# A four-layer convolution and attention chain: 64-output products in column halves, one instruction order to the end, and later corner arithmetic

## The chip, the cores and the metric

The kernel runs on one core of one Trainium2 chip. The metric is the device time of one execution in microseconds. Before the change three runs took 5382.01, 5395.89 and 5406.22 us; the median is 5395.89.

## What is computed

The input x is a batch of 2 images of 256 channels and 64 x 64 pixels, all in fp32. Four layers follow each other.

```python
# layer 0: group norm, 4-head attention over the 4096 pixels, projection
xn = group_norm(x); q, k, v = w_qkv @ xn
attn = softmax(q.T @ k * 64**-0.5);  x = xn + w_proj @ (attn @ v) + b_proj
# layer 1: position term
x = x + pos_embedding
# layer 2: bottleneck with a modulated deformable 3x3 convolution, 256 -> 64 -> 64 -> 256
h = relu(bn1(w1 @ x))
off, mask = conv3x3(h, woff)            # 18 offsets and 9 masks per pixel
samp = bilinear(h, pixel + tap + off) * sigmoid(mask)
h = relu(bn2(w2 @ samp));  x = relu(bn3(w3 @ h) + x)
# layer 3: two deformable 3x3 convolutions of 256 channels, with group norm and residual
h = relu(group_norm(x));  h = deform_conv(h, dw1, pw1, w1)
h = relu(group_norm(h));  x = x + deform_conv(h, dw2, pw2, w2)
```

## The kernel before

A batch has 4096 pixels, cut into NB = 8 blocks of 512. The program has two large parts.

**Attention** (line 160 on) goes through four units: two batches by two pairs of heads. A unit has 256 score tiles, each 128 queries by 1024 keys. The loop handles two tiles, n and n+1, per turn: scores of the tiles ahead (L569, TensorE), their row maxima (L581, VectorE), the exponentials (L587, ScalarE), 16 transposes of a finished tile (L599, TensorE) with two copies out of PSUM (L616 VectorE, L618 ScalarE), and the products with the values (L628, TensorE). Sixteen tiles make a block of 256 queries. Its four partial outputs are put together in `combine` (L508 to L514, on GpSimd), with factors `f` that go through DRAM (L498, L502). Two blocks make 512 queries, so 32 tiles are the period of the work around them. `project` (L533) then adds the projection to the residual, and, after the second pair of heads, `second_layer` calls `first` (L891).

Everything else in attention is background work, put between the tiles at due steps, or one step at a time from generators that `background` advances. A generator that yields "any", "a", "b" or True has used the turn; one that yields False passes it to the next generator. The background consists of:

- `first(b, i, ...)` (L891, L903): the product w1 of 64 outputs for one pixel block, and its copies to `h` with a row above and below.
- `before(b, ...)`: the transposed image of `h` in DRAM (L920, copy L924, four stores L929), the offset convolution (L938, copies L954 and L956, transposes by products L966), and the corner arithmetic (`corners`, L722 to L760), which yields gather indices `bidx` and weights `bw`. For batch 0 it runs in unit 1 and for batch 1 in unit 3.
- `conv(b, ...)`: gathers of four corners for each pixel and tap (L817 on GpSimd's queue), weighting (L1009, VectorE), sums (L1019, L1020, on GpSimd for batch 0 and on VectorE for batch 1), transposes (L1030), `second` (the product w2 of 64 outputs, L1039, five groups of taps), and `third` (the product w3, L1052, then L1056, L1059 and L1060 on VectorE). For batch 0 it runs in unit 2 and the start of unit 3.
- `early_image` (L1112 to L1134): batch 0's layer-3 image is written to DRAM; each block is loaded with `bott.block` (L873).

**Deform** (line 1138 on) is layer 3. Each step gathers four corners of 256 channels (L817, `four`), weights and adds them (L1305 ScalarE, L1311 VectorE), transposes (L1323), copies (L1332) and multiplies by the weights (L1342). The offsets come from `offsets`: weights `wf` (L1190, VectorE), products `pd` (L777, TensorE), a copy, shift products (L794), another copy (L803), transposes by products (L808) and the corner arithmetic. `conv` of batch 1 runs beside the first 160 or so steps; its gathers and layer 3's share GpSimd's queue.

**Order.** Both parts open a `manual_schedule` region of their own. Within a region TensorE, ScalarE, VectorE and GpSimd issue instructions in the order in which the program emits them. SP's queue is left to the scheduler, and so is the way in which the two regions' instructions are merged on one engine. PSUM for background work is one buffer, `pm`: the helper `ps` gives it out and first emits the copies that were put off for its previous use.

Of the kernel before, what the change touches and what calls it, by code (L numbers as in the profile page):

```python
# [18 lines left out]
P = 128  # L19
# [3 lines left out]
CM = 64  # L23
# [37 lines left out]
class Net:  # L61
# [39 lines left out]

    def zero_borders(self, zero):
# [67 lines left out]
    def attention(self, bott):  # L170
# [5 lines left out]
        with ExitStack() as ctx:  # L176
# [15 lines left out]
            engines = mybir.EngineType  # L192
            ctx.enter_context(
                tc.manual_schedule(
                    engines={engines.PE, engines.Activation, engines.DVE, engines.Pool}
                )
            )
# [241 lines left out]
            class Block:  # L439
# [66 lines left out]
                def combine(self):  # L506
                    o = self.o
                    nc.gpsimd.tensor_mul(o, o, self.f)  # L508
# [316 lines left out]
    class Bottleneck:  # L825
# [52 lines left out]
        def first(self, b, i, x, pools, ps):  # L878
# [10 lines left out]
            pc = ps([P, 512])  # L889
            for cb in range(2):  # L890
                nc.tensor.matmul(  # L891
                    pc[:CM], lhsT=self.w1[:, cb, :], rhs=x[:, cb, :],
                    start=(cb == 0), stop=(cb == 1),
                )
            where = [(rows(i), 1, 0, 8)]
# [5 lines left out]
            def copy():  # L901
                for dst, r, r0, n in where:
                    nc.scalar.activation(  # L903
                        dst[:, r * W : (r + n) * W], pc[:CM, r0 * W : (r0 + n) * W], AF.Relu,
                        scale=s[:CM, 0:1], bias=t[:CM, 0:1],
                    )
# [4 lines left out]
        def before(self, b, pools, ps):  # L911
# [5 lines left out]
            def image(i):  # L917
# [7 lines left out]
                for r in range(2):  # L925
                    for s in range(2):
                        y0 = 8 * i + r + 1 - s
                        dst = img[y0 : y0 + 7 : 2, 1 : W + 1, s, :].rearrange("j x c -> x j c")
                        nc.sync.dma_start(dst, t[64 * r : 64 * r + 64, :, :])  # L929

            def offsets(i):
# [29 lines left out]
                yield "any"  # L961
# [23 lines left out]
        def conv(self, b, pools, ps):  # L985
# [49 lines left out]
            def second(sts):  # L1035
                out = ps([P, 512])
                for g, st in enumerate(sts):
                    n = CM * len(self.GROUPS[g])
                    nc.tensor.matmul(  # L1039
                        out[:CM], lhsT=self.w2[:n, g, :], rhs=st[:n], start=(g == 0), stop=(g == 4)  # L1040
                    )
# [29 lines left out]
            for n, (i, g, js) in enumerate(steps):  # L1071
# [14 lines left out]
                if g == 4:  # L1086
                    del self.idx[b, i]
                    todo.append((n + 3, lambda sts=sts, h2=h2: h2.append(second(sts))))
                    for ob in range(2):

                        def out(i=i, ob=ob, x=x, h2=h2):
                            third(i, ob, h2[0], x)
# [4 lines left out]
                        todo.append((n + 4 + ob, out))  # L1097
# [5 lines left out]
    def early_image(self, bott, pools, ps):  # L1103
# [33 lines left out]
    def deform(self, bott):  # L1137
# [5 lines left out]
        with ExitStack() as ctx:  # L1143
# [10 lines left out]
            engines = mybir.EngineType  # L1154
            ctx.enter_context(
                tc.manual_schedule(
                    engines={engines.PE, engines.Activation, engines.DVE, engines.Pool}
                )
            )
# [381 lines left out]
```

## Time and profile before

| | us |
|---|---|
| median of three runs | 5395.89 |
| profiled execution | 5241.94 |
| its span, first to last instruction | 5240.2 |
| TensorE busy | 4868.1 (93%) |
| VectorE busy | 4207.5 (80%) |
| ScalarE busy | 2815.3 (54%) |
| GpSimd busy | 2246.8 (43%) |

The mean granted TensorE clock is 0.975. The profile names engines PE (TensorE matmuls), PEld (TensorE weight loads), DVE (VectorE), ACT (ScalarE), POOL (GpSimd) and SP (the DMA queue of SyncE); an ending q means the engine's queue or sequencer. Of the chain of work that ended last 65% lies on TensorE and 16% on VectorE. The costliest groups are L1311 on VectorE (1610.9 us), L587 on ScalarE (1145.9), L1342 on TensorE (1240.7) and L817 on GpSimd, as two groups of gathers (1155.0 and 580.2). In order of time attention ends near 2985 us, the last gather of layer 2's batch 1 is used near 3620, and the rest is layer 3.

### The profile page before, as it was taken

The page shows a single profiled execution, that of the slowest core. Times are in us where ns is not written, and L with a number is a line of the kernel's source. Part 1 is how long each engine was busy: PE and PEld are TensorE (multiplying, and loading weights), DVE is VectorE, ACT ScalarE, POOL GpSimd, SP SyncE. Part 2 cuts the span into 40 slices and gives each one's busy share as a digit, 9 for nine tenths or more (in the row PEclk, how much of TensorE's full clock was granted, in tenths as well). Part 3 has the DMA queues.
Part 4 walks back from the last instruction along what each step waited for, and adds up shares of the span by engine and source line. Part 5 has one row for each costly group of instructions (what it writes and reads, how often), then busy time and mean ns, then how long its engine had stood idle before and what let it go on. Part 6 is the DMA issues. An engine that isn't in the chain of part 4 may idle for free.

```text
span 5240.2 us, 99232 instructions
## 1 busy us (share of the span) xinstructions
PE 4868.1 (93%) x37976; PEld 2657.6 (51%) x37976; DVE 4207.5 (80%) x7922; ACT 2815.3 (54%) x5189; POOL 2246.8 (43%) x2241
## 2 busy tenths in 40 slices
PE   8999999999999999999999866667999999999998
PEld 5555565555555555655555523333444444444443
DVE  6878767787677787677677577777999999999998
ACT  5676656666566666666666422223444544444444
POOL 0111100010016676463000177776566566666665
PEclk9999999999999999999999988888999999999999
DMA  5221111111113333322511266667999999999998
GB/s 170 63 94 56 44 66 44 44 36 41 51 50 96 92 98 93 99 82 76 142 34 30 85 208 223 217 221 277 367 325 331 353 364 353 350 391 347 346 349 320
DMA packets 347147, 920.40 MB, mean 176 GB/s; under 512 B 58716, under 2 KB 98458, under 8 KB 346670
## 3 DMA queue, kind: packets, MB, share of 16 engines
q0 software_dynamic: 194688, 683.85, 36.8%
q1 hardware_dynamic: 151982, 230.20, 14.0%
q8 instruction: 298, 4.88, 0.4%
q14 instruction: 179, 1.47, 0.1%
HBM read 815.90 MB, written 89.60 MB: 173 GB/s over the span
## 4 chain that ended last, share of the span: by engine, by line
PE 65%; DVE 16%; DMA 6%; issue 6%; ACT 5%; POOL 3%; SPq 0%; ACTq 0%; DVEq 0%; POOLq 0%
PE av L628 15%; PE sc L569 14%; PE out L1342 10%; PE tt L599 9%; DVE smp L1311 8%; PE pd L777 5%; DMA four<-img,didx 4%; PE pt L1323 3%; POOL bfour L817 2%; DVE low L581 2%; ACT e L587 2%; PE pm L1039 1%; PE pm L271 1%; PE pm L533 1%; DMA bfour<-img,bidx 1%
## 5 line engine op out<-in xcount | busy, mean ns | idle before, releaser
L1311 DVE SCALAR_TENSOR_TENSOR smp<-four,dw,smp 128x256 f32<-128x256 f32 x3456 | 1610.9, 483 | 203.0 <-ACT smp L1305 120.3
L587 ACT ACTIVATE e<-sc,low 128x1024 f32<-128x1024 f32 x1024 | 1145.9, 1119 | 783.5 <-DVE low L581 780.4
L817 POOL DMA_INDIRECT four<-img,didx x1152 | 1155.0, 1003 | 665.5 <-DVE smp L1311 325.4
L1342 PE MATMUL out<-st,wc 128*128 128x512 f32 x2304 | 1240.7, 621 | 173.9 <-ACT st L1332 145.9
L581 DVE TENSOR_REDUCE low<-sc 128x1 f32<-128x1024 f32 x1024 | 1204.2, 1217 | 236.6 <-PE sc L569 234.0
L628 PE MATMUL av<-et,v 128*64 128x256 f32 x8192 | 1006.6, 386 | 0.0
L569 PE MATMUL sc<-k,qs 64*128 64x512 f32 x2048 | 998.4, 606 | 0.6 <-ACT e L587 0.3
L569 PE MATMUL sc<-k,q 64*128 64x512 f32 x2048 | 979.8, 605 | 0.0
L508 POOL TENSOR_TENSOR o<-o,f 128x1024 f32<-128x1024 f32 x64 | 151.6, 2369 | 1882.9 <-DVE o L463 872.5
L599 PEld LDWEIGHTS tt<-ident,e 64*128 64x128 f32 x16384 | 652.8, 139 | 526.9 <-issue 277.4
L1305 ACT ACTIVATE smp<-four,dw 128x256 f32<-128x256 f32 x1152 | 523.3, 503 | 460.4 <-DMA four<-img,didx 392.2
L599 PE MATMUL tt<-ident,e 64*128 64x64 f32 x16384 | 726.5, 226 | 47.1 <-DVE et L616 22.3
L618 ACT COPY et<-tt 128x512 f32<-128x512 f32 x1152 | 658.1, 584 | 166.5 <-PE tt L599 164.9
L616 DVE COPY et<-tt 128x512 f32<-128x512 f32 x896 | 611.0, 682 | 156.1 <-PE tt L599 155.9
L628 PEld LDWEIGHTS av<-et,v 128*64 128x64 f32 x8192 | 556.6, 137 | 308.6 <-issue 58.8
L1323 PEld LDWEIGHTS pt<-ident,smp 128*128 128x128 f32 x2304 | 321.8, 145 | 749.3 <-issue 426.2
L1332 ACT COPY st<-pt 128x1024 f32<-128x1024 f32 x288 | 290.7, 1009 | 722.0 <-PE pt L1323 722.0
L817 POOL DMA_INDIRECT bfour<-img,bidx x576 | 580.2, 1007 | 193.7 <-issue 93.2
L1342 PEld LDWEIGHTS out<-st,wc 128*128 128x128 f32 x2304 | 392.6, 197 | 437.6 <-issue 208.2
L1323 PE MATMUL pt<-ident,smp 128*128 128x128 f32 x2304 | 458.7, 282 | 72.9 <-DVE smp L1311 67.3
L777 PE MATMUL pd<-x,wf 128*126 128x512 f32 (+2 forms) x896 | 460.0, 599 | 10.6 <-DMA x<-xn 10.3
L569 PEld LDWEIGHTS sc<-k,qs 64*128 64x128 f32 x2048 | 346.1, 188 | 215.1 <-issue 118.1
(160 smaller groups left out, 3383.8 us busy)
## 6 DMA issues: line engine op xcount, KB each, us to landing
f<-share_d SPq DMA_DIRECT2D x128, 256.0 KB, 4.0
xb<-xn SPq DMA_DIRECT2D x55, 512.0 KB, 3.4
img<-imgt SPq DMA_DIRECT2D x96, 256.0 KB, 9.3
four<-img,didx POOLq DMA_INDIRECT x1152, 6.1
xa<-res SPq DMA_DIRECT2D x32, 512.0 KB, 2.9
xb<-in_x SPq DMA_DIRECT2D x20, 512.0 KB, 4.6
bfour<-img,bidx POOLq DMA_INDIRECT x576, 3.1
qs<-q SPq DMA_DIRECT2D x64, 128.0 KB, 2.2
```

Of the source, the lines that this page charges most:

```text
L569: nc.tensor.matmul(s[:, j, :], lhsT=q[u, i // 2][int(h != j)][halves[j], at : at + P], rhs=k[u][c][halves[j], h, :], start=True, stop=True,)
L581: nc.vector.tensor_reduce(low, s, AX.X, ALU.max, negate=True)
L587: nc.scalar.activation(e.rearrange("p j n -> p (j n)"), s, AF.Exp, bias=blk.low[:, g, c : c + 1], accum_out=blk.sum[:, g, c : c + 1],)
L599: nc.tensor.transpose(pt[:, m, :], e[half, m // 4, m % 4 * P : m % 4 * P + P], self.ident[half, half],)
L616: nc.vector.tensor_copy(dst, pt)
L618: nc.scalar.copy(dst, pt)
L628: nc.tensor.matmul(now["av"][halves[h], :], lhsT=v[u][c][:, m, halves[h]], rhs=ets[j][:, m, h, :], start=(m == 0), stop=(m == 7),)
L777: nc.tensor.matmul(pd[:m, r0 * W : r1 * W], lhsT=wt(s, t), rhs=src[:, (y + r0) * W : (y + r1) * W], start=(n == 0), stop=(n == len(srcs) * ...
L817: self.nc.gpsimd.indirect_dma_start(out=dst, out_offset=None, in_=img, in_offset=bass.IndirectOffsetOnAxis(ap=idx, axis=0),)
L1311: nc.vector.scalar_tensor_tensor(smps[s], four[:, c], weight(s, c), smps[s], ALU.mult, ALU.add)
L1323: nc.tensor.transpose(pts[u][:, c, j * P : (j + 1) * P], smp[:, c * P : c * P + P], self.ident,)
L1342: nc.tensor.matmul(outs[ob], lhsT=wc[k][:, c, ob * P : ob * P + P], rhs=sts[u][:, c, :], start=(k == 0 and c == 0), stop=(k == K2 - 1 and ...
```

## The change

1. In `first` and `second` the 512 columns are split into two halves of 256. The second half's 64 outputs go to the upper 64 partitions of a 256-column PSUM tile. Their copies become one activation per half, with scale and bias copied to the upper partitions at the start.
2. One `manual_schedule` region in `run` replaces the two, so the order of emission holds from attention's start to the end.
3. `combine` of the last block of the last unit runs on VectorE.
4. In `before`, corner arithmetic waits for 6 turns passed on (batch 1) or 1 (batch 0) in place of one used turn, and each image waits for one more. The last image's two stores for s = 1 go to ScalarE's DMA queue.
5. `third` is split: the product and L1056 in one step, L1059 and L1060 as `fourth` in the next.
6. `early_image` loads a block while the one before it is handled.

```diff
+        for v in (self.bn_s, self.bn_t):
+            nc.vector.tensor_copy(v[CM:P, 0:2], v[0:CM, 0:2])
...
-            engines = mybir.EngineType
-            ctx.enter_context(
-                tc.manual_schedule(
-                    engines={engines.PE, engines.Activation, engines.DVE, engines.Pool}
-                )
-            )
...
                 def combine(self):
+                    end = self.u + 1 == len(units) and self.i == 15
+                    engine = nc.vector if end else nc.gpsimd
                     o = self.o
-                    nc.gpsimd.tensor_mul(o, o, self.f)
-                    nc.gpsimd.tensor_add(o[:, 0:2], o[:, 0:2], o[:, 2:4])
+                    engine.tensor_mul(o, o, self.f)
+                    engine.tensor_add(o[:, 0:2], o[:, 0:2], o[:, 2:4])
...
-                    nc.gpsimd.tensor_add(self.av[:, half : half + 256], o[:, 0], o[:, 1])
+                    engine.tensor_add(self.av[:, half : half + 256], o[:, 0], o[:, 1])
...
-            pc = ps([P, 512])
+            pc = ps([P, 256])
             for cb in range(2):
-                nc.tensor.matmul(
-                    pc[:CM], lhsT=self.w1[:, cb, :], rhs=x[:, cb, :],
-                    start=(cb == 0), stop=(cb == 1),
-                )
-            where = [(rows(i), 1, 0, 8)]
+                for j in range(2):
+                    nc.tensor.matmul(
+                        pc[CM * j : CM * j + CM],
+                        lhsT=self.w1[:, cb, :],
+                        rhs=x[:, cb, 256 * j : 256 * j + 256],
+                        start=(cb == 0),
+                        stop=(cb == 1),
+                    )
+            where = [(rows(i), 1, 0, 4), (rows(i), 5, 4, 4)]
...
-                        dst[:, r * W : (r + n) * W], pc[:CM, r0 * W : (r0 + n) * W], AF.Relu,
-                        scale=s[:CM, 0:1], bias=t[:CM, 0:1],
+                        dst[:, r * W : (r + n) * W], pc[p, r0 * W : (r0 + n) * W], AF.Relu,
+                        scale=s[p, 0:1], bias=t[p, 0:1],
...
-                        nc.sync.dma_start(dst, t[64 * r : 64 * r + 64, :, :])
+                        queue = nc.scalar if b == 1 and i == NB - 1 and s else nc.sync
+                        queue.dma_start(dst, t[64 * r : 64 * r + 64, :, :])
...
                 yield "any"
-                yield "any"
+
+                for _ in range((1, 6)[b]):
+                    yield False
                 while len(self.idx) == self.CORNERS:
...
                 while self.blocks[b] <= i:
                     yield False
+                yield False
                 image(i)
...
             def second(sts):
-                out = ps([P, 512])
+                out = ps([P, 256])
                 for g, st in enumerate(sts):
                     n = CM * len(self.GROUPS[g])
-                    nc.tensor.matmul(
-                        out[:CM], lhsT=self.w2[:n, g, :], rhs=st[:n], start=(g == 0), stop=(g == 4)
-                    )
+                    for j in range(2):
+                        nc.tensor.matmul(
+                            out[CM * j : CM * j + CM],
+                            lhsT=self.w2[:n, g, :],
+                            rhs=st[:n, 256 * j : 256 * j + 256],
+                            start=(g == 0),
+                            stop=(g == 4),
+                        )
...
-                ps.later(
-                    lambda: nc.scalar.activation(
-                        h2, out[:CM], AF.Relu, scale=s[:CM, 1:2], bias=t[:CM, 1:2]
-                    )
-                )
+                def copy():
+                    for j in range(2):
+                        p = slice(CM * j, CM * j + CM)
+                        nc.scalar.activation(
+                            h2[:, 256 * j : 256 * j + 256], out[p], AF.Relu,
+                            scale=s[p, 1:2], bias=t[p, 1:2],
+                        )
+
+                ps.later(copy)
...
-                xs = x[:, ob, :]
-                nc.vector.scalar_tensor_tensor(
-                    xs, pc, s[:, 2 + ob : 3 + ob], xs, ALU.mult, ALU.add
-                )
+                nc.vector.scalar_tensor_tensor(
+                    x[:, ob, :], pc, s[:, 2 + ob : 3 + ob], x[:, ob, :], ALU.mult, ALU.add
+                )
+
+            def fourth(i, ob, x):
+                xs = x[:, ob, :]
                 nc.vector.tensor_scalar(xs, xs, t[:, 2 + ob : 3 + ob], 0.0, ALU.add, ALU.max)
                 nc.vector.bn_stats(self.stats[b][:, ob, i, :], xs)
...
-                        todo.append((n + 4 + ob, out))
+                        todo.append(
+                            (n + 4 + 2 * ob, lambda i=i, ob=ob, x=x, h2=h2: third(i, ob, h2[0], x))
+                        )
+                        todo.append((n + 5 + 2 * ob, out))
...
+        ahead = bott.block(pools["x"], x2d, 0)
         for i in range(NB):
-            x = bott.block(pools["x"], x2d, i)
+            x = ahead
+            if i < NB - 1:
+                ahead = bott.block(pools["x"], x2d, i + 1)
...
     def run(self):
         with ExitStack() as ctx:
             bott = self.Bottleneck(ctx, self)
+            engines = mybir.EngineType
+            ctx.enter_context(
+                self.tc.manual_schedule(
+                    engines={engines.PE, engines.Activation, engines.DVE, engines.Pool}
+                )
+            )
             self.attention(bott)
             self.deform(bott)
```

More of the change, by code (lines that the diff above doesn't have):

```diff
@@ L902, in copy @@
                 for dst, r, r0, n in where:
+                    p = slice(0, CM) if r0 < 4 else slice(CM, P)
+                    r0 %= 4
                     nc.scalar.activation(
-                        dst[:, r * W : (r + n) * W], pc[:CM, r0 * W : (r0 + n) * W], AF.Relu,
-                        scale=s[:CM, 0:1], bias=t[:CM, 0:1],
+                        dst[:, r * W : (r + n) * W], pc[p, r0 * W : (r0 + n) * W], AF.Relu,
+                        scale=s[p, 0:1], bias=t[p, 0:1],
                     )
@@ L1089, in conv, with out @@
                     for ob in range(2):
-                        def out(i=i, ob=ob, x=x, h2=h2):
-                            third(i, ob, h2[0], x)
+                        def out(i=i, ob=ob, x=x):
+                            fourth(i, ob, x)
                             if ob == 1:
@@ L1153, in deform @@
             pop = ctx.enter_context(tc.tile_pool(name="df_po", bufs=1, space=PSUM))
[L1154 to L1159, printed above, removed]
             T = DWK * DWK
```

## The prediction

> **What bounds the kernel now.** I read the page's slices first, then the busy times by stretch, then the order of time at the places that the change touches. The profiled execution took 5241.94 us (span 5240.2).
>
> ```profile
> PE   8999999999999999999999866667999999999998
> POOL 0111100010016676463000177776566566666665
> PEclk9999999999999999999999988888999999999999
> ```
>
> Each digit is one fortieth of the span, 131 us. TensorE is full everywhere but in slices 23 to 28 (about 2960 to 3660 us), where its granted clock is lower too. The stretches (columns: length, then busy time with the number of instructions of PE, PEld, DVE, ACT and POOL, then clock, DMA share, GB/s):
>
> ```profile
> 700.00:1400.00 700.00, 697.25 (x7642) 414.88 (x7639) 531.40 (x809) 446.77 (x835) 67.70 (x46) 1.00 0.15 44
> 1640.00:2260.00 620.00, 603.21 (x6309) 351.76 (x6310) 474.71 (x639) 390.47 (x727) 395.96 (x443) 1.00 0.31 94
> 2540.00:2960.00 420.00, 407.23 (x4303) 243.27 (x4303) 308.07 (x483) 277.93 (x520) 39.10 (x27) 0.99 0.18 47
> 3100.00:3660.00 560.00, 391.61 (x1113) 177.71 (x1114) 430.70 (x989) 153.65 (x268) 416.60 (x407) 0.84 0.70 232
> ```
>
> Attention is bound by TensorE: 97 to 99.6%, so TensorE time taken out there comes off the span. From 3013 to 3620 the bound is POOL: it issues one gather after another, 0.95 us each with 0.30 between that is put down to issue, and in order of time no gap above 0.45 us appears until 3623. There TensorE time is worth nothing. After 3660 TensorE leads again, with code the change leaves alone.
>
> **The column halves.** Three rows price them:
>
> ```profile
> 3003.75 1.93 PE L891 MATMUL pm<-res,w 128*64 128x512 f32 x4
> 2237.65 4.65 PE L1039 MATMUL pm<-bst,w 128*64 128x512 f32 x10 [0.63 <-ACT bst L1032]
> 2265.05 1.95 PE L628 MATMUL av<-et,v 128*64 128x256 f32 x16
> ```
>
> An fp32 product of 64 outputs by 512 columns is two instructions of 0.427 us, start to start (4.65 for ten). The attention's av products already have the form that the change introduces: 64 outputs, 256 columns, alternating between the two halves of the output partitions; sixteen take 1.95 us, so a pair takes about 0.213 and the halves run beside each other. L891 goes from 4 x 0.427 to 4 pairs x 0.213: 0.86 us less. L1039 goes from 10 x 0.427 to 10 pairs x 0.213: 2.13 less. A rule speaks against it: the Trainium skill, TensorEngine Tiling (Array Packing), "Instruction Overhead", puts about 60 cycles on every matmul, an estimate of 25 ns at the 2.4 GHz of its TensorE page. By that, 4 more instructions cost 0.10 and 10 more 0.25, leaving 0.76 and 1.88. The av row has its instructions' overhead in it, so I take 0.86 and 2.13. Fifteen L891 groups lie in full attention (the sixteenth in the tail below): 15 x 0.86 = 12.9. Eight L1039 groups (batch 0) lie there: 8 x 2.13 = 17.1. The other eight are under POOL's gathers: nothing. By the rule the two sums are 11.4 and 15.0. Bounds: 0 if halves run one after the other, 30 by the av row. Taken: **30.0**.
> The evacuations get one more ScalarE instruction each (64x512 becomes two of 64x256; 0.39 us is the price of the smallest form here); ScalarE is 63% busy beside it. Doubled weight loads run on PEld, 57% busy there. The two constant copies fall into the first 65 us, where DVE is busy 25. Nothing for these; without that cover 23 x 0.39 = 9 us.
>
> **Corners later.** The corner arithmetic of batch 1 now meets GpSimd's combination:
>
> ```profile
> 2942.22 2.34 POOL L508 TENSOR_TENSOR o<-o,f 128x1024 f32<-128x1024 f32 x1 [40.29 <-DVE pos L731]
> 2942.23 2.39 DVE L733 CAST whole<-pos 128x72 int32<-128x72 f32 x1
> 2944.65 1.30 DVE L736 CAST floor<-whole 128x72 f32<-128x72 int32 x1
> 2947.45 1.11 PE L599 MATMUL tt<-ident,e 64*128 64x64 f32 x15 [3.36 <-DVE et L616]
> 3015.35 0.20 DVE L733 CAST whole<-pos 128x72 int32<-128x72 f32 x1
> ```
>
> The same cast takes 2.39 us beside a POOL product and 0.20 alone (last row). VectorE's next copy of et is queued behind it, and TensorE waits 3.36 us. In the changed order corners come at tile 24 of each 32 in place of 19 (a tile is 2.7 us), past the combination at 20. What that is worth comes from equal blocks of batch 0 in unit 1, where corners stand at 22 and TensorE has no such wait: the chain of waits has L938 at 1214.93 and 1301.60, a block of 86.67; in unit 3, L271 at 2761.02 and 2849.84, a block of 88.82. 2.15 x 6 blocks = **12.9** (bounds 5 and 17). The image's step back by one turn moves its four stores on SP and one transpose group, not its length.
>
> **Image input ahead, and third split.**
>
> ```profile
> 2535.70 1.52 ACT L1112 ACTIVATE bx<-bx,gn_sh,gn_sc 128x512 f32<-128x512 f32 x2 [4.89 <-DMA bx<-x2d]
> 2537.74 1.59 PE L599 MATMUL tt<-ident,e 64*128 64x64 f32 x16 [4.98 <-ACT et L618]
> ```
>
> The load came too late once; ScalarE and then TensorE stood 4.98 us. In the new SP order each load stands a block earlier, ahead of the previous block's image stores. **5.0** (0 to 7). Splitting third puts L1056 on one step and L1059/L1060 (0.49 and 0.69) on the next, so that et copies aren't queued behind all three. In 1640 to 2260 TensorE idles 16.8 us from several causes; I take **3** (bounds -5 and 8: shifted steps can meet the combination anew).
>
> **One order to the end, last combination on VectorE, ScalarE's queue.** Before, the deformable layer's first work was woven into attention's tail:
>
> ```profile
> 2992.26 7.44 PE L777 MATMUL pd<-x,wf 128*126 128x512 f32 x12 [10.28 <-DMA x<-xn]
> 2999.62 1.08 PE L533 MATMUL pm<-avs,wproj 128*64 128x512 f32 x4
> 3012.97 1.03 POOL L817 DMA_INDIRECT bfour<-img,bidx  x1 [20.86 <-DMA img<-imgt]
> 3022.18 0.23 DVE L722 TENSOR_TENSOR pos<-pd,base 128x72 f32<-128x72 f32 x1 [1.82 <-PE pd L808]
> 3048.89 0.94 POOL L817 DMA_INDIRECT four<-img,didx  x1 [0.30 <-issue]
> ```
>
> The last projection stood behind twelve pd products. Now: factors land about 2984.4 (POOL's old start); three VectorE operations, an estimate of 2.4 from DVE rows of the same sizes (0.68 for 512, 0.42 for 256, about 1.25 for 1024); two projections with their additions, to 2990.6; L891 in halves, three activations, transposes, copy, to 2994.3; two image stores on SP beside two on ScalarE; landed about 2998. The 28 first gathers could start **15 us earlier**, and at 1.28 each end at 3034 against 3048.9.
> But the same order puts wf (3.43 on VectorE) and pd behind both corner blocks. From 2994.3: L938 2.8, its copies 2.1, L966 1.0, corners 4.0; the second block's L938 overlaps, then copies 2.1, L966 1.0, corners 4.0: 3011.7. Half of wf, 1.7; 28 pd instructions. TensorE idles before them, and the Trainium skill (TensorE: Matmul & The Clock Gate, "The HAM clock gate") says an idle window of about 3.4 us halves its clock until it has been busy as long: 8 instructions in 3.4 us and 20 x 0.427, 11.9. The row has 12 in 7.44, then 16 x 0.44: 14.5. I take the row. Then wide copy, shift products, od and sel: 5.9. L722 would run at about 3034, against 3022.18. On VectorE all but one of the early bfour sums are queued behind L722, and a gather of step 9 onward needs a buffer that these sums free: gathers 21 to 28 go out one or two per freed buffer, until 13.8 us after L722. The first four leaves about 3048, **1 us** earlier (bounds -8 and 14, the latter if POOL alone decides; by the rule 3.6). POOL's stage then moves as a whole.
> At its end POOL stood 8.01 us (3623.69) behind the last L1056; its L1039 is 2.1 shorter: **2** (0 to 5).
>
> **Sum.** 30.0 + 12.9 + 5.0 + 3 + 1 + 2 = 53.9 us off 5241.94: 5188. The median of the runs is 5395.89, 154 us above the profiled execution, for which the page shows no cause; I carry the gain over in proportion (x 1.029): 55.5, so 5340.
>
> **Rivals.**
> - *The halves don't overlap* (weight loads or a drain between them). For it: PEld loads double. Against: the av row. Then 23.9 x 1.029 = 25: 5371, within 0.5%. Chance 0.10.
> - *VectorE and ScalarE swallow half of the products' gain*: ACT waits for low 163 us in 1640 to 2260. Against: TensorE is 97% busy there all the same. 54 - 15 = 39: 5356. Chance 0.17.
> - *POOL alone decides the tail*: gathers at 3034, 13 us more: 5326. For it: the stage is POOL's. Against: the VectorE queue above. Chance 0.15.
> - *Slower: sums late for their transposes.* The batch 0 transposes wait for GpSimd's sums; one did, 1.82 us at 1657.73, behind the combination. Forty are in unit 2, and all move. At 1.82 each, 30 of 40 cancel the 54; stalls of 3 us at all forty give 120 - 54 = 66 slower: 5464. Against: only one stalls now, and the lag between sum and transpose is unchanged. Chance 0.06.
> - *My forecast*: 0.52.
>
> A measurement of this kernel tells about 0.5% (27 us) from no change. Faster by more 0.82 (forecast, swallowed half, POOL's tail, less their lower ends), within 0.11, slower 0.07. The range 5295 to 5378 goes from 1.9% below to just short of the rival in which halves don't pay plus the runs' own spread of 12 us.
>
> **What would show it.** L1039 as twenty instructions in about 2.4 us, L891 as eight in 1.1; blocks of unit 3 at 86 us or less; L733 at 0.2 there; no wait of ScalarE for bx; first bfour near 2998 less the attention's gain, first four some 36 to 50 later; POOL gapless in between or with a hole before gather 21. Wrong if the halves take 4 us, if TensorE's idle time in unit 2 grows over 17 us, or if the stage from the first four to the last L1039 gets longer than 576 us.

## The result and the profile after

| | before, us | after, us | ratio (95% interval) |
|---|---|---|---|
| the recorded comparison, 6 runs each | 5392.94 (5378.87 to 5406.22) | 5336.88 (5331.80 to 5348.98) | 0.9901 (0.9881 to 0.9922) |
| again, where before takes 5241 (5 runs of after) | 5240.94 | 5195.80 (5190.19 to 5203.13) | 0.9915 (0.9901 to 0.9929) |
| again, where before takes 5393 (5 runs of after) | 5393.46 | 5349.37 (5332.42 to 5358.58) | 0.9908 (0.9893 to 0.9922) |

The change made the kernel about 1% faster; 5340 had been predicted. The absolute times come in two sorts. On some chips before takes about 5242 us and on others about 5393. The profile of before (5241.94) was of the first sort, the profile taken of the changed kernel (5333.18) of the second. Each ratio below is of runs on one chip.

The page's slices of the changed kernel's first profile are these, each digit a fortieth of the span (133 us), in tenths.

```profile
PE   8999999999999999999999655566999999999998
...
POOL 0111101000027777461000566674566566666664
PEclk9999999999999999999999777788999999999999
```

Slices 23 to 28 are emptier than before, although nothing in the change makes the gathers slower. The stretches of the same profile, and below them those of the changed kernel on the other sort of chip (`a1_after`), show what the change did and what the chip did (columns: length, busy time with instructions of PE, PEld, DVE, ACT and POOL, then clock, DMA share, GB/s).

```profile
1640.00:2260.00 620.00, 604.24 (x6509) 358.63 (x6505) 480.15 (x655) 404.04 (x751) 405.16 (x452) 1.00 0.33 95
...
3100.00:3660.00 560.00, 325.55 (x1034) 145.18 (x1034) 373.99 (x861) 128.23 (x239) 379.24 (x371) 0.78 0.62 197
```

```profile
700.00:1400.00 700.00, 694.42 (x7728) 415.48 (x7726) 539.48 (x814) 453.93 (x845) 68.40 (x47) 1.00 0.16 45
1640.00:2260.00 620.00, 606.58 (x6561) 360.15 (x6557) 486.85 (x663) 405.77 (x756) 407.49 (x452) 1.00 0.33 98
2540.00:2960.00 420.00, 404.79 (x4302) 241.72 (x4302) 292.71 (x481) 275.63 (x516) 44.28 (x35) 0.97 0.19 55
3100.00:3660.00 560.00, 380.25 (x1266) 185.56 (x1266) 433.39 (x998) 171.27 (x299) 408.18 (x398) 0.83 0.74 245
```

In the gather stage (3100 to 3660) all engines together do less in the first profile: PE 326 us in place of 380, POOL 379 in place of 408, at 197 GB/s in place of 245. The last section comes back to that. To find what the change did, `a1_after` is set beside `b0_before`, a profile of before on a chip of the same sort. A unit is counted from the start of the last copy of partial sums (`o<-av` on VectorE, L463 before, L460 after) of one to that of the next, and attention ends with the last of them.

| us | before | after | difference |
|---|---|---|---|
| start to end of unit 0 | 753.9 | 754.9 | +1.0 |
| unit 1 | 713.9 | 710.8 | -3.1 |
| unit 2 | 761.4 | 741.0 | -20.4 |
| unit 3 | 755.8 | 728.2 | -27.6 |
| attention's end to the first gather `four` | 67.2 | 71.3 | +4.1 |
| first `four` to the last `second` | 571.7 | 573.4 | +1.7 |
| last `second` to the end | 1619.0 | 1614.4 | -4.6 |
| span | 5243.0 | 5194.0 | -49.0 |

(The other profile of before has 758.2 for unit 2: repeats lie some 3 us apart.) All of the gain was made in attention, 50.1 us of it, and the tail gave 4.1 back.

### The profile page after: what moved, and what is told of

Its sections match the earlier page's. It is cut to its first block, busy times and chain, and to the rows that moved or that the text cites. A ratio compares the mean times of both kernels' runs of the same rounds, so it can differ in the third digit from the quotient of the medians.

```text
span 5331.4 us, 99714 instructions
## 1 busy us (share of the span) xinstructions
PE 4839.4 (91%) x38200; PEld 2655.5 (50%) x38200; DVE 4190.9 (79%) x7927; ACT 2822.3 (53%) x5221; POOL 2238.2 (42%) x2238
## 4 chain that ended last, share of the span: by engine, by line
PE 37%; DVE 13%; issue 6%; another core or an unknown queue 3%; ACT 3%; POOL 2%; DMA 2%; SPq 0%; DVEq 0%; ACTq 0%; POOLq 0%
PE out L1365 11%; DVE smp L1334 8%; PE pd L777 6%; PE av L628 5%; PE sc L569 5%; PE tt L599 3%; PE pt L1346 3%; POOL bfour L817 1%; DVE bfour L1020 1%; DVE low L581 1%; DMA four<-img,didx 1%; PE pd L794 1%; ACT st L1355 1%; ACT smp L1328 1%
## 5 line engine op out<-in xcount | busy, mean ns | idle before, releaser
L628 PE MATMUL av<-et,v 128*64 128x256 f32 x8192 | 994.9, 385 | 0.0
```

The source lines that it names most:

```text
L628: nc.tensor.matmul(now["av"][halves[h], :], lhsT=v[u][c][:, m, halves[h]], rhs=ets[j][:, m, h, :], start=(m == 0), stop=(m == 7),)
```

## The experiments

The three runs of unchanged kernels come first. They are the ones that the others are measured against.

`b0_before` is before itself: 5244.72 us, span 5243.0.

> The kernel before, profiled once more, because its first profile (5242 us) lies 150 us below its own median while the changed kernel's profile (5333) lies on its median. Theory A: ordinary runs of the kernel before lose those 150 us in the stage of layer 2's batch-1 gathers, where the changed kernel's profile shows every engine at rest together for 7 to 30 us, waiting for something the profile can't name: then attention ends again at 2982 +- 2 us, the stretch from the first layer-3 gather to the last w2 product is 640 us or more (576 in the first profile), and the whole is 5380 to 5405. Theory B: the loss is spread over the execution (a lower clock): then attention ends 60 us or more later and the stretch stays below 600.

It was on a chip where before takes 5242 again (attention's end at 2985.0, the stage from the first `four` 571.7), so it tests neither theory on what the slower runs lose.

`a0_after`, the changed kernel on a chip where before takes 5393: 5349.37, ratio 0.9908.

> The changed kernel again, to stand beside the versions with one part undone. If a part's worth can be read as a difference on one chip: attention ends near 2949 as in its first profile, 7 us before the full-width version (2956.7) and 10 us before the version with early corners (2959.3); the whole is near 5207 where the kernel before takes 5242, and slower than the version with two regions (5191). If instead the ratio of the first measurement (0.990) holds here: 5190, and attention has to end 15 us before 2949 or the tail has to be shorter, because nothing waits unexplained here.

`a1_after`, the changed kernel where before takes 5241: 5195.80, ratio 0.9915.

> The changed kernel, unchanged, beside the two-region version on one chip. Theory A (one order costs the tail): attention ends within 5 us of the two-region version, the first gather of layer 3 (`four`) starts 71 to 74 us after attention's end against 63 to 66 there, and the whole is 7 to 12 us slower than with two regions. Theory B (one order changes attention too): attention also ends 7 to 13 us later than with two regions, and the whole is 15 to 22 us slower. Theory C (the tail is made good by POOL's stage): the two differ by under 3 us.

### Full width again, in the changed kernel

```diff
-                for j in range(2):
-                    nc.tensor.matmul(
-                        pc[CM * j : CM * j + CM],
-                        lhsT=self.w1[:, cb, :],
-                        rhs=x[:, cb, 256 * j : 256 * j + 256],
...
+                nc.tensor.matmul(
+                    pc[:CM], lhsT=self.w1[:, cb, :], rhs=x[:, cb, :],
...
```

(and the same in `second`)

> The changed kernel with the two 64-output products back in full width (512 columns, one half of the partitions, one activation each). The prediction's sum: attention ends 30 us later than the changed kernel's 2949.4, near 2979, and the whole is 30 us slower, near 5367, nothing of it from the gather stage. Rival, half swallowed: PE saves 30 us of products but waits more for the copies of the transposed tiles; attention ends near 2962 (12 us later) and the whole is 10 to 15 us slower unless the gather stage adds its own.

Measured: 5221.76 (5218.15 to 5226.72), ratio 0.9963 (0.9949 to 0.9976), against 0.9915 with the halves. Units 1 to 3 took 715.1, 749.5 and 738.7 us, so against `a1_after` the halves are worth 4.3, 8.5 and 10.5 us there, 23.3 together, and 26.0 by the medians (the two runs are of two chips, on which before takes 5242 and 5241). The prices of one group are as they were read from the av row. In order of time on TensorE, `a1_after` (L1051) and the first profile after (L893) have

```profile
2222.13 2.48 PE L1051 MATMUL pm<-bst,w 128*64 128x256 f32 x20
```

```profile
1119.23 1.08 PE L893 MATMUL pm<-res,w 128*64 128x256 f32 x8
```

Twenty instructions in 2.48 us where ten took 4.65, eight in 1.08 where four took 1.93: the two halves of the output partitions do run beside each other. That the whole is 23.3 and not the 30.0 that these prices give is not in the products themselves. Over units 1 to 3 (columns as above) `a1_after` has the first of these lines and `e1_full_width` the second:

```profile
754.90:2934.90 2180.00, 2141.93 (x23292) 1282.11 (x23292) 1667.46 (x2507) 1448.01 (x2696) 702.89 (x729) 1.00 0.24 68
```

```profile
753.40:2956.70 2203.30, 2171.50 (x23152) 1284.58 (x23152) 1664.38 (x2507) 1435.80 (x2673) 700.40 (x729) 1.00 0.24 68
```

TensorE's busy time is 29.6 us shorter, nearly the 30.0, but its idle time grew by 6.3, from 31.8 to 38.1. Of this, 5.3 us are waits for ScalarE's copies to `h` (L910). `e1_full_width` has no such wait of TensorE, and `a1_after` has these in attention (columns: what was waited for, us in total, times, longest):

```profile
PE pm L491 <- ACT h L910: 2.4, 9, 0.3
PE pm L1153 <- ACT h L910: 1.0, 1, 1.0
PE pm L287 <- ACT h L910: 1.0, 1, 1.0
PE pm L1073 <- ACT h L910: 0.9, 1, 0.9
```

They are products of other background work that use the buffer `pm` next, and the copies to `h` have to leave it first.

### The halves alone, in before

```diff
+        for v in (self.bn_s, self.bn_t):
+            nc.vector.tensor_copy(v[CM:P, 0:2], v[0:CM, 0:2])
...
-            pc = ps([P, 512])
+            pc = ps([P, 256])
...
-                out = ps([P, 512])
+                out = ps([P, 256])
```

(with the products and copies in halves, as in the change, and nothing else of it)

> The kernel before with nothing but the column halves (and the two constant copies they need). The prediction's sum: 13 us in the w1 products and 17 in unit 2's w2 products, attention ends at 2953 +- 3 in place of 2983, the whole is 30 us faster, 5212. Rival, swallowed: TensorE then waits for the copies of the transposed tiles (PE before L599) for half of it or more; attention ends at 2968 or later, the whole is 8 to 15 us faster, and the stage of batch-1 gathers stays at 572 +- 3 us.

> The halves alone, once more, for a profile to set beside before's units (713.9, 761.4 and 755.8 us from last partial sum to last partial sum of units 1, 2 and 3). In the first run of it unit 1 took 717.5, unit 2 757.8 and unit 3 755.7; the changed kernel's unit 2 took 758.8 beside it and 741.0 on another chip, so 18 us of unit 2 may be the chip's. Theory A (halves lose in units 1 and 3 to the image's wait for h, and pay in unit 2): if before takes about 5242 on this chip, unit 1 is 717 to 718, unit 2 739 to 745, unit 3 755 to 756, attention ends near 2968, ratio 0.996 to 0.998. Theory B (halves pay nowhere without the later image): unit 2 takes 755 or more on such a chip too, attention ends near 2984, ratio 0.999 or more.

Measured: 0.9977 (0.9963 to 0.9991) and 0.9989 (0.9981 to 0.9996), both on chips where before takes 5393. That is 6 to 12 us, far from 30. Unit 1 took 717.5 us in both, 3.6 more than before, and unit 3 took 755.7 and 756.2, no less than before's 755.8. Unit 2 took 757.8 and 759.6. It takes 758.8 in `a0_after` too and 741.0 in `a1_after`, so its length on these chips says nothing of the halves, and these two runs do not settle the second run's theories on unit 2. Another run speaks for the first: `e3_corners_early` (below) has the halves with corners and image at their old turns, where before takes 5242, and its unit 2 takes 742.0, within the first theory's 739 to 745. It also has the split and the loading ahead, but these change unit 2 by 1.0 us only (759.8 without them, 758.8 with them, in `e6_no_split_no_ahead` and `a0_after`). On units 1 and 3 the first theory is confirmed. The waits of attention in `e10_halves_again`, where L929 is the image's transposes and L912 the copies to `h` (L920 and L903 before), have

```profile
PE pm L929 <- ACT h L912: 20.3, 14, 2.3
```

Before has 1.7 us in two such waits. One of the 14 in order of time, in the same kernel:

```profile
1120.47 1.08 PE L895 MATMUL pm<-res,w 128*64 128x256 f32 x8
...
1123.33 1.96 ACT L912 ACTIVATE h<-pm,bn_t,bn_s 64x256 f32<-64x256 f32 x4
...
1125.35 0.40 PE L929 MATMUL pm<-ident,h 64*128 64x64 f32 x3 [1.43 <-ACT h L912]
```

and the same place in `b0_before`:

```profile
1121.33 1.35 ACT L903 ACTIVATE h<-pm,bn_t,bn_s 64x512 f32<-64x512 f32 x3
...
1122.74 0.40 PE L920 MATMUL pm<-ident,h 64*128 64x64 f32 x3
```

ScalarE's copies to `h` are four instructions of 1.96 us in place of three of 1.35, and the transposes of the image come right behind them on TensorE, which stands still. TensorE gains 0.85 on the product and gives 1.43 back; that is 0.6 us a block, the 0.61 by which the copies are longer, and six such waits make up the 3.6 us of unit 1. The Trainium skill states this in TensorEngine Tiling (Array Packing), "PSUM Bottleneck": packing the array speeds up TensorE but not the copies out of PSUM, which may then bind. Here they bind where TensorE stands directly behind them, although ScalarE as a whole was busy only 63 to 66% in attention's stretches of before.

### The halves and the image one turn later, in before

```diff
                 while self.blocks[b] <= i:
                     yield False
+                yield False
                 image(i)
```

> Before with the column halves and, of the later order, only the image's one turn. Halves alone ended attention at 2984.7, no earlier than before, with 18 us of TensorE waits of the image's transposes for ScalarE's last copy of h. Theory A (these waits ate the halves' gain): the transposes wait under 4 us in all, attention ends at 2966 to 2973, and the ratio to before is 0.994 to 0.996. Theory B (the halves' gain in attention is eaten by slower steps elsewhere, not by this wait): the wait goes but attention ends at 2980 or later, ratio 0.997 or more.

Measured: 5204.92 (5201.48 to 5207.70), ratio 0.9931 (0.9917 to 0.9945). That is 36 us, above the 21 to 31 of theory A, and theory B is out; no wait of the transposes for `h` is left. (Other products still wait for these copies, 8.0 us in attention against 1.0 with the halves alone.) (Attention's end at 2942.0 is far before A's 2966 to 2973, since those were counted from 2984.7 of a chip whose unit 2 is 17 us longer.) Units 1 to 3 took 711.8, 740.7 and 734.5 us. The one `yield False` takes 5.7 us from unit 1 and 21 from unit 3 (against the halves alone; these two units take the same in `a0_after` and `a1_after` within 0.7 us, so they can be set beside each other across the chips). More than went with the waits for `h` was gained, and the next two experiments show what else.

### The later order alone, and the later order taken out

In before, at full width, the corners and the image are made later:

```diff
                 ps.later(lambda: copy((0, 1)))
                 yield "any"
-                yield "any"
+
+                for _ in range((1, 6)[b]):
+                    yield False
...
+                yield False
                 image(i)
```

> Before with only the later corners and the later image: full width, two regions, no split, no loading ahead, combination on GpSimd. By the prediction's term it takes 12.9 us off: attention ends near 2970, unit 3's blocks take 86 to 87 us (88.8 before), ratio 0.9975. If the image's turn alone matters when there are halves, and the corners' term is as sized, the same. If the corners' term was too large (corners meet the combination elsewhere), attention ends at 2976 or later and the ratio is 0.999 or more.

Measured: 5226.84 (5221.83 to 5234.72, 9 runs), ratio 0.9977 (0.9967 to 0.9987): 14.1 us where 12.9 had been predicted, and unit 3's equal blocks take 86.7 us (88.8 before). Its profile, the fastest of the nine runs, has unit 3 at 743.5, some 12 us less than before, and unit 2 at 750.2, 8 to 11 us less. The prediction has no term for unit 2. There the two edits overlap: the later order alone brings it to 750, the halves without it to 742.0 (`e3_corners_early`), both to 741. Then the opposite, both edits taken out of the changed kernel:

```diff
-
-                for _ in range((1, 6)[b]):
-                    yield False
+                yield "any"
...
-                yield False
                 image(i)
```

> The changed kernel with corner arithmetic and images at their old turns (one used turn, no turn passed on). The prediction's sum: the corners of batch 1 meet GpSimd's combination again, 2.15 us in each of six blocks, attention ends 13 us later, near 2962, and the whole is 13 us slower. Rival: with halves and split steps the positions have shifted anyhow and the meeting does not recur: attention ends within 3 us of 2949.4.

Measured: 5219.38 (5215.31 to 5222.37), ratio 0.9955 (0.9941 to 0.9969): 21 us slower than the changed kernel by the ratios, 23.6 by the medians, where 13 had been expected, and unit 3's blocks take 89.4 to 89.7 us. In order of time on GpSimd, VectorE and TensorE, `e3_corners_early` has

```profile
2651.57 2.35 POOL L508 TENSOR_TENSOR o<-o,f 128x1024 f32<-128x1024 f32 x1 [42.56 <-DVE o L460]
...
2652.28 1.69 DVE L731 TENSOR_SCALAR pos<-pos 128x72 f32<-128x72 f32 x1
...
2654.01 1.31 DVE L733 CAST whole<-pos 128x72 int32<-128x72 f32 x1
...
2655.97 0.71 PE L599 MATMUL tt<-ident,e 64*128 64x64 f32 x15 [1.53 <-DVE et L616]
```

and the halves with the image's turn alone, `e7_halves_image_later`, where the same lines are L511, L734 and L736,

```profile
2647.71 2.35 POOL L511 TENSOR_TENSOR o<-o,f 128x1024 f32<-128x1024 f32 x1 [40.96 <-DVE o L466]
...
2652.73 0.19 DVE L734 TENSOR_SCALAR pos<-pos 128x72 f32<-128x72 f32 x1
...
2652.95 0.20 DVE L736 CAST whole<-pos 128x72 int32<-128x72 f32 x1
```

In `e3_corners_early` the corner arithmetic runs into GpSimd's product, and the two instructions shown take 1.69 and 1.31 us; TensorE then waits 1.53 for VectorE. In `e7_halves_image_later` the offsets come after the image, so its one turn has carried the corners along: from L734 on they run 2.7 us after GpSimd's product ended and take 0.19 and 0.20. Unit 3's blocks are 86.4 us there and 86.2 in the changed kernel. **The image's one turn is enough for both jobs**: it frees the transposes from the copies to `h`, and it moves the corners off the combination. The corners' own further turns save another 0.2 us a block and the one meeting that is left in `e7_halves_image_later` (L736 takes 1.31 us at 2907.5, and TensorE waits 1.52). The corners' turns without the image's, and the image's turn at full width, were not run.

### No split of third, no loading ahead

```diff
-            x = ahead
-            if i < NB - 1:
-                ahead = bott.block(pools["x"], x2d, i + 1)
+            x = bott.block(pools["x"], x2d, i)
...
-                        todo.append((n + 5 + 2 * ob, out))
+                        todo.append((n + 4 + ob, out))
```

(and L1082 and L1083 back in `third`)

> The changed kernel without the split of the w3 step and without the image input a block ahead. The prediction's sum: 5 us for the input, 3 for the split: attention ends 8 us later than the changed kernel's. In the profile ScalarE waits about 5 us for bx once again. Rival: the loads are hoisted by the scheduler of SP's queue anyhow and the wait falls elsewhere; attention ends within 2 us of the changed kernel's.

Measured: 5360.85 (5356.85 to 5376.45), ratio 0.9943 (0.9930 to 0.9957), against 5349.37 and 0.9908 of `a0_after` on the same chip: the two edits together are worth 11.5 us, where 8 had been expected, and 12.7 in unit 3 (741.0 against 728.3). In order of time `e6_no_split_no_ahead` still has before's late load, and `a0_after` the rest of it:

```profile
2538.20 1.52 ACT L1133 ACTIVATE bx<-bx,gn_sh,gn_sc 128x512 f32<-128x512 f32 x2 [4.58 <-DMA bx<-x2d]
```

```profile
2529.51 1.52 ACT L1141 ACTIVATE bx<-bx,gn_sh,gn_sc 128x512 f32<-128x512 f32 x2 [1.19 <-DMA bx<-x2d]
```

The load's wait costs more than itself. Behind it TensorE stood 4.68 us, and from 2538 to 2544 its granted clock in `e6_no_split_no_ahead` was 0.50, some 3 us more (an estimate, half of the 6); `a0_after` has 1.00 in all of 2520 to 2560. Over unit 3 `e6_no_split_no_ahead` has the first of these lines and `a0_after` the second:

```profile
2225.50:2966.50 741.00, 714.57 (x7588) 428.56 (x7584) 543.64 (x851) 497.12 (x923) 183.82 (x187) 0.98 0.24 68
```

```profile
2224.40:2952.70 728.30, 709.98 (x7586) 425.69 (x7582) 542.24 (x852) 497.12 (x923) 183.60 (x187) 1.00 0.25 69
```

Of the 12.7 us, 8.1 are idle time of TensorE (26.4 and 18.3), and 4.6 are longer work at a lower clock. The two edits were not run apart, so how the rest divides between them stays open. Nor is it certain that they bring this much without the corners' own turns. `e7_halves_image_later` has neither the two edits nor those turns, and its unit 3 takes 734.5, 6.5 us less than here. It differs from `e6_no_split_no_ahead` in the order to the end as well, but with two regions or one the changed kernel's unit 3 lies between 728.2 and 731.8. So the split and the loading ahead probably make good in part what the corners' turns cost.

### Two regions again, in the changed kernel

```diff
     def run(self):
         with ExitStack() as ctx:
             bott = self.Bottleneck(ctx, self)
-            engines = mybir.EngineType
-            ctx.enter_context(
-                self.tc.manual_schedule(
...
```

(and a region each for attention and deform, as before)

> The changed kernel with a region of fixed order for each part again, so that the deformable layer's first products can be woven into attention's tail. The prediction: the tail's two effects cancel, the first layer-3 gather leaves 1 us later than in the changed kernel (72 us after attention's last copy), the whole is unchanged within 5 us. Rival, fixed order costs: woven in, wf and pd run during the projection's waits and keep TensorE's clock up; the first layer-3 gather leaves 55 to 62 us after attention's last copy, the whole is 10 to 17 us faster. A third possibility, that the new position of the gathers sets the stalls of the stage: then the stage's length changes by tens of us with attention unchanged.

> The changed kernel with the two regions of before. Its ratio to before is 0.990 by the earlier run of it; under A the changed kernel's ratio beside it is 0.9915 to 0.9925, under B 0.993 to 0.994, under C within 0.0006 of it. In the profile: first gather of `four` some 64 us after attention's end, and L722 some 43 us after it.

Measured: 5191.03 (5186.05 to 5192.77), ratio 0.9899 (0.9884 to 0.9914), and 5189.04 (5183.25 to 5193.77), ratio 0.9900 (0.9884 to 0.9915). Beside the second run the changed kernel took 5195.80. The intervals overlap; the two profiles show where the 6.8 us between the medians lie. Attention ends at 2934.8 and 2934.9, the stage from the first `four` on takes 573.6 and 573.4, and between the two the first `four` starts after 63.9 us with two regions and after 71.3 in one order. The changed kernel's tail in order of time:

```profile
2940.43 1.97 PE L533 MATMUL pm<-avs,wproj 128*64 128x512 f32 x4 [5.54 <-DVE avs L514]
...
2945.94 1.98 PE L893 MATMUL pm<-res,w 128*64 128x256 f32 x8 [0.79 <-DVE res L544]
...
2950.77 5.43 PE L946 MATMUL pm<-h,woff 64*96 64x512 f32 x6 [0.52 <-DVE imgt L931]
...
2975.35 12.78 PE L777 MATMUL pd<-x,wf 128*126 128x512 f32 x28 [5.06 <-DVE wf L1213]
...
2985.50 0.95 POOL L817 DMA_INDIRECT bfour<-img,bidx  x1 [0.30 <-issue]
...
2992.72 0.23 DVE L722 TENSOR_TENSOR pos<-pd,base 128x72 f32<-128x72 f32 x1 [15.05 <-PE pd L808]
...
2995.32 0.94 POOL L817 DMA_INDIRECT bfour<-img,bidx  x1 [8.88 <-DVE floor L740]
```

With two regions (pd is L783, the projection L539):

```profile
2945.30 2.05 PE L783 MATMUL pd<-x,wf 128*126 128x512 f32 x2 [10.57 <-DMA x<-xn]
2947.28 1.97 PE L539 MATMUL pm<-avs,wproj 128*64 128x512 f32 x4
...
2951.57 1.08 PE L539 MATMUL pm<-avs,wproj 128*64 128x512 f32 x4
...
2954.38 1.08 PE L899 MATMUL pm<-res,w 128*64 128x256 f32 x8
```

The stretch from 2951 to 2975 us, first in one order, then with two regions:

```profile
2951.00:2975.00 24.00, 14.22 (x28) 6.35 (x28) 9.40 (x43) 3.17 (x6) 10.93 (x12) 0.50 0.62 209
```

```profile
2951.00:2975.00 24.00, 21.76 (x78) 8.63 (x76) 7.26 (x27) 5.05 (x9) 9.30 (x10) 0.99 0.62 196
```

With two regions the pd products are woven between the projections. TensorE first stands 10.57 us, longer than in one order, but from then on it works almost without a gap, and its granted clock is 0.99 in this stretch. So the second projection and `first` run at 1.08 us, and the offsets are ready in time: GpSimd issues its 28 gathers from 2962.96 to 2998.7 without a hole. In one order TensorE stands 5.54 us before the projection, its clock is 0.50 all through the stretch, everything up to `first` takes twice its time (1.98 in place of 1.08), and pd starts at 2975.35 only. VectorE's sums are queued behind L722, and gather 21 waits 8.88 us for the buffer that one of them frees. (The profile names L740; the first of these sums, L1031, ended at 2995.05, 0.27 before the gather.) One order costs 7.4 us of tail, as theory A of `a1_after` had it; the whole is 6.8 slower, just under its 7 to 12. (The first run with two regions has 64.1 us, and the five other profiles in one order have 71.9 to 73.4.) The version with two regions is the fastest seen.

## Why the prediction was right, step by step

| step | predicted, us | measured, us |
|---|---|---|
| halves | 30.0 | 23.3 in units 1 to 3, 26.0 by medians, with the rest of the change in place; 6 to 12 alone |
| corners (and image) later | 12.9 | 14.1 at full width, 21 to 24 with the halves |
| image input ahead, third split | 5.0 + 3 | 11.5 |
| one order, combination, ScalarE's queue | 1 | -4.1 (-7.4 for the order, 3.3 for the rest) |
| end of the gather stage, and after it | 2 | 2.9 |
| sum | 53.9 | 49.0 in the profiled spans, 45.1 by the medians beside them |

The steps were measured one at a time with different edits beside them and do not add: in units 1 and 3 the halves and the image's turn pay together, in unit 2 they overlap. That the sum came so close is in part luck: the halves and the tail were put too high by 4 to 7 and by 5 us, the later order and the image input too low by 1 to 11 and 3.5. The 56.1 us of the recorded comparison beside the predicted 55.5 are luck too, since the two repeats gave 45.1 and 44.1.

**The halves' prices were right, their cover was not.** The row of av gave 0.86 and 2.13, and the groups measured 0.85 and 2.17 less. By the estimate from the 60 cycles that the Trainium skill puts on each matmul (TensorEngine Tiling (Array Packing), "Instruction Overhead") the big group would have been 4.65 - 1.88 = 2.77 us; it took 2.48, as the row said. What failed is the step that cost the doubled activations at nothing because ScalarE is 63% busy. A share of busy time hides an added instruction only where nobody stands directly behind it. At the image's transposes TensorE did, for 20.3 us. In the changed kernel most of this cover was restored by the image's turn, by a step to which the prediction gave no value of its own ("not its length"). The shortfall that is left, 6.7 us, is mostly the same step: 5.3 of it are waits of other products for the same copies. Of the eight L1039 groups five fell into unit 2 and three into unit 3, not eight into unit 2, which alters no sum. The rival in which half of the gain is swallowed named the right engine, ScalarE, for a kernel without the image's turn.

**Corners later was right in mechanism and close in size, but the edit that it gave no value was enough.** L733 fell to 0.20 us and the blocks from 88.8 to 86.2, as listed. With the image's turn alone they are at 86.4. The gain in unit 2 was not foreseen.

**Input ahead and split** were undersized by 3.5 us within their bounds; ScalarE's wait for `bx` fell to 1.19. The term for the load priced the wait and not the half clock behind it, which was in the prediction's own row: 16 transposes took 1.59 us there and take 0.71 elsewhere.

**The tail has the failed step.** L722 was put at about 52 us after attention's end (2982.0 in that profile) and the first `four` at 66; they came at 57.8 and 71.3. The hole before gather 21 is where it was foretold. Two terms were mis-sized. From the projections to pd TensorE ran at half its speed, behind an idle time of 5.54 us (L533 1.97, L893 1.98, and the six products of each offset convolution 5.43 and 5.19 where 2.8 was put): 3 x 0.9 + 2 x 2.5 = 7.7 us more than put. The Trainium skill's rule (TensorE: Matmul & The Clock Gate, "The HAM clock gate") was weighed for pd alone, where it gave 11.9 and the row 14.5; the trace has 12.78 there, nearer to the rule. Applied from the projections on it would have found a good half of the 7.7 (an estimate: 2.7 for the three short groups and 1.7 for the first convolution). By the rule the clock comes back after about 3.4 us of work, while here six products ran for 5.43 us on end and it stayed at 0.50; the measurement decides. And the two pairs of stores, from issue at 2950.74 to the gather at 2960.72, took 10.0 us where 3.7 was put; with two regions, issued at 2958.26, they took 4.7. So the first `bfour` came 25.8 us after attention's end, 5 to 6 earlier than before (31.3), and not 15. The rival in which POOL alone decides is out: before gather 21 POOL waited for VectorE. (The sum from 2994.3 to the second block's corners gives 3011.3 and not 3011.7, which alters nothing.)

**The proportion.** The gain was scaled by 1.029 for the slower median. Where before takes 5393 the gain was 56.1 and 44.1 us, where it takes 5241 it was 45.1: the runs show no such proportion. That adds 1.6 us to 53.9, so it didn't matter.

**What was listed as proof of error.** The halves do not take 4 us but 2.48. TensorE's idle time from 1640 to 2260 us, 16.8 before, is 15.8 in the first profile after and 13.4 in `a1_after`, not over 17. "The stage longer than 576 us" is met by the first profile (655.3) and by `a0_after` (668.1) and not by `a1_after` (573.4). `e10_halves_again` has 681.6, with before's order and regions, so the chip makes the difference and not the change.

## What to carry to other kernels

When a product is made shorter by splitting its output, look for who stands directly behind the copies of that output; if it is the bounding engine, move it by one turn, which here was worth as much as the products (27 us in units 1 and 3). Value each edit together with the edits that restore its cover: alone the halves brought 6 to 12 us, with one added `yield False` 36 (on the other sort of chip). TensorE's last work before the change of stage ran at half clock here, behind 5.54 us of idle time, so leave other work woven into such a tail, as the two regions did.

## What the runs showed of the hardware

**Stalls of all engines that come with the chip.** On chips where before takes 5393, the gather stage took 655.3 us in the changed kernel's first profile, 668.1 in `a0_after`, 670.4 in `e6_no_split_no_ahead`, and 673.9 and 681.6 in the two runs of the halves alone; on the others it took 569 to 574 in all nine profiles, before's two among them. In order of time the changed kernel's first profile has

```profile
3069.84 0.94 POOL L817 DMA_INDIRECT four<-img,didx  x1 [0.30 <-issue]
3074.88 1.01 ACT L1355 COPY st<-pt 128x1024 f32<-128x1024 f32 x1 [16.42 <-remote]
3074.97 0.23 DVE L722 TENSOR_TENSOR pos<-pd,base 128x72 f32<-128x72 f32 x1 [11.58 <-remote]
...
3077.57 1.15 POOL L817 DMA_INDIRECT bfour<-img,bidx  x1 [6.79 <-DVE bsmp L1031]
```

and its waits have

```profile
ACT st L1355 <- remote: 125.2, 13, 20.5
ACT bst L1043 <- remote: 109.7, 9, 30.8
```

"Remote" is a release that the profile can't place. ScalarE and VectorE stand for 16.42 and 11.58 us and are let go within 0.1 us of each other, 4 us after GpSimd's gathers ran out. Such waits sum to 422 us over the engines of this profile, and to 0 in every profile on the other chips. Attention has few of them (9.2 us), but unit 2, where batch 0 gathers, takes 755 to 760 us in all five profiles from there, and 740 to 741 in the kernels with the halves and the image's turn on the others. `a0_after` is 162.8 us longer than `a1_after`: 17.8 in unit 2, 94.7 in the gather stage and 48.3 behind it. The 150 us between before's profile and its median probably divide alike, but no profile of before was taken on such a chip. What the chips differ in was not tried and stays open.
